# Row sums of attention weights by two adding transfers instead of matmuls with ones, and a new place for what uses them

## The chip, the cores and the metric

The kernel runs on one core of a Trainium2 chip. The time is that of the device, in microseconds, of one execution of the whole program; the median of three runs stands for a kernel. A core has TensorE (PE in the profile, with its weight loads as PEld), VectorE (DVE), ScalarE (ACT), GpSimd (POOL) and SyncE (SP), which here issues the transfers. Each engine works through its own list of instructions in order; they wait for each other through semaphores. Sixteen DMA engines move data between the on-chip memory and the device memory.

## The reference

Two layers over `x` of 16 batches, 1024 rows, 256 columns, all in float32. The first layer multiplies by a normalised adjacency matrix, then has two dense products with batch norms, a residual sum and a layer norm. The second, which the change is in, is attention:

```python
c_adj = jnp.mean(fea, axis=1)                     # of the rows, fea = x transposed
diff = c_adj[:, None, :] - c_adj[:, :, None]
A = jnp.abs(jnp.abs(jax.nn.sigmoid(diff) - 0.5) - 0.5) * 2.0
A_s = (A + jnp.transpose(A, (0, 2, 1))) * 0.5
g = jnp.einsum('bcn,bnm->bcm', fea, adj[None, :, :] * A_s)
q = relu(g * para)                                # in 4 heads of 64
k, v = x @ kv_w                                   # in 4 heads of 64
attn = jax.nn.softmax(jnp.einsum('bhnd,bhmd->bhnm', q, k) * scale, axis=-1)
out = jnp.einsum('bhnm,bhmd->bhnd', attn, v)
x = _layernorm(x + out, axis=-1)
```

The softmax needs, for each query and head, the sum of 1024 exponentials. That sum is what the change computes in another way.

## The kernel before: the parts concerned

The attention stage goes through 256 steps `g`, 16 a batch. Four steps make a turn; a turn is one half of the queries (`hf`, 512 of them) with one pair of heads, so a batch has four turns. A step makes scores for two blocks of 128 keys (`s`), takes their exponentials (`e`), adds these into `acc` and multiplies them by the values (`o`):

```python
def scores(g):
    ...
        t = ps_s.tile([P, 2, FB], F32, tag="s", name=f"s{g}_{a}")      # two buffers, a step fills both
        ... nc.tensor.matmul(t[...], kTs[...], qTs[...], start=True, stop=True)

def exps(g):
    for a in range(2):
        E[g, a] = ep.tile([P, 2, FB], F32, tag="e", name=f"e{g}_{a}")  # six buffers
        nc.scalar.activation(E[g, a], S.pop((g, a)), AF.Exp)

def sums(g):
    ...
    if cp == 0:
        ACC[b, hf, pair] = accp.tile([P, 2, FB], F32, tag="acc", name=f"acc{g}")
        nc.vector.tensor_add(ACC[b, hf, pair], E[g, 0], E[g, 1])
    else:
        for a in range(2):
            nc.vector.tensor_add(ACC[b, hf, pair], ACC[b, hf, pair], E[g, a])
```

`acc` then still has 128 partial sums, one a partition, for each query and head. `dens` adds them with matmuls by a block of ones, once per half, in the first matmuls of the next turn:

```python
def dens(b, hf):
    p = ps_t.tile([P, FB], F32, tag="t", name="pd")
    for pair in range(NP):
        acc = ACC.pop((b, hf, pair))
        for h in range(2):
            k = 32 * (2 * pair + h)
            ... nc.tensor.matmul(p[k : k + 32, :], ones32, t[:, h, :], ...)
    DT[b, hf] = otp.tile([P, FB], F32, tag="dt", bufs=1, name=f"dt{b}_{hf}")
    nc.scalar.copy(DT[b, hf], p)
    if not by_pe(b, hf):
        for k in range(HEADS):
            put_o(b, hf, slice(C + k * DR, C + (k + 1) * DR), DT[b, hf][32 * k : 32 * k + DR, :])
```

The outputs and the sums (`DR = 8` equal rows a head) go to device memory and come back in blocks (`fetch_o`, tile `ob`), so that a transposition in 32x32 blocks brings them into rows. `finish_a` does that for 256 queries (in this text: a finished pair, of two row blocks), divides, adds the residual and takes the moments; `finish_b` normalises and stores:

```python
def finish_a(b, j):
    ...
        t = pool_r[0].tile([P, 2, CD], F32, tag=pool_r[1], name=f"r_{b}_{j}")       # CD = C + HEADS * DR
        nc.vector.transpose(
            t.rearrange("p a c -> p (a c)"), OB.pop((b, j)).rearrange("p a c -> p (a c)")
        )
        nc.vector.reciprocal(rd, t[:, :, C:].rearrange("p a (h r) -> p a h r", r=DR)[:, :, :, 0])
        p = r = t[:, :, :C]
    ...
        nc.vector.tensor_mul(r..., p..., rd...)
    nc.vector.tensor_add(r, r, x1s.pop((b, j)))
    mv, rs = ln_stats(sm, r, f"z{b}_{j}")
    ...
```

The first layer's result for later batches is prepared in the same turns: `bn2_q` (GpSimd, tile `yt`), `rows` and `ln1_a` (VectorE: `x`, `mv_a`; then GpSimd: `rs_a`, `nm_a`), `ln1_b` (ScalarE, `x`). Keys (`pk`), values (`pv`) and the graph product (`pg`, whose results become `qT`) of the next batch fill TensorE at the front of a turn.

A table says at which half turn each piece is put out: `put(b, t, f, ...)` at half turn `t` of batch `b` (eight a batch), `between[k]` after step `k`. The pieces of both half turns stand ahead of the turn's steps:

```python
for t in range(...):
    g = NK * t
    now = [p for s in (2 * t, 2 * t + 1) for p in [(opening, (s,))] + arrange(at.get(s, []))]
    behind = max((k + 1 for k, fa in enumerate(now) if is_short(fa)), default=0)
    for k in range(len(now) + 1):
        if k == behind and 0 <= g < nsteps:
            sums(g)
        if k < len(now):
            f, a = now[k]
            f(*a)
    for k in range(g, g + NK):
        if 0 <= k + 1 < nsteps:
            scores(k + 1)
            exps(k + 1)
        if 0 <= k < nsteps:
            if k > g:
                sums(k)
            attend(k)
        for f, a in between.pop(k, ()):
            f(*a)
```

`dens` is one of the short pieces, so in a turn with `dens` the first addition `sums(g)` stands behind it.

Of the kernel before, what the change touches and what calls it, by code (L numbers as in the profile page):

```python
# [9 lines left out]
F32 = mybir.dt.float32  # L10
AF = mybir.ActivationFunctionType
OP = mybir.AluOpType
AX = mybir.AxisListType
# [3 lines left out]
P = 128  # L17
# [5 lines left out]
def gnn_norm_attention_kernel(  # L23
# [16 lines left out]
    nc = tc.nc  # L40
    B, N, C = x.shape
# [5 lines left out]
    NH = N // FB  # L47
# [33 lines left out]
    Q = 32  # L81
# [1 line left out]
    y_blk = [yT_all[b].rearrange("i (d e) (q n) -> q e (i d) n", e=Q, q=NQ) for b in range(B)]  # L83


    DR = 8
    CD = C + HEADS * DR
    o_dram = {(b, h): dram.tile([NT // NH, CD, P], F32, name=f"o{b}_{h}") for b in range(B) for h in range(NH)}
    x1_dram = {
# [39 lines left out]
    with ExitStack() as l0:  # L129
# [33 lines left out]
        with ExitStack() as ph1:  # L163
# [9 lines left out]
            for i in range(0, NT, 2):  # L173
                t = hp.tile([P, 2, N], F32, tag="h", name=f"A{i}")
# [29 lines left out]
            for h in range(NH):  # L204
                rows = range(h * KB, (h + 1) * KB)
# [10 lines left out]
                for j in range(NT):  # L216
                    p = ps.tile([P, FB], F32, tag="ah"[j % 2], name="pat")
                    for k, i in enumerate(rows):
                        nc.tensor.transpose(p[:, ts(k, P)], A[i][:, ts(j, P)], ident)
                    dst, acc = AhT[:, j, ts(h, FB)], col[:, h, j : j + 1]  # L220
# [22 lines left out]
            for c in range(HT):  # L243
                p = ps.tile([P, FB], F32, tag="a", name="pw1")
# [3 lines left out]
            for c in range(CT):  # L248
                p = ps.tile([P, FB], F32, tag="a", name="pw2")
# [149 lines left out]
            for f in range(HT):  # L399
                for h in range(NH):  # L400
# [3 lines left out]
                    p = hidden(B - 1, h, f)  # L404
# [5 lines left out]
        right = lambda name, bufs: ctx.enter_context(tc.tile_pool(name=name, bufs=bufs, side="right"))  # L410
        keep = right("keep", 1)
        ldp = right("ldp", LDP)
        accp = right("accp", 2)
        RD = keep.tile([P, B * NT + 1, HEADS], F32, name="RD")
        ones32 = keep.tile([P, 32], F32, name="ones32")
        stq = keep.tile([P, 2, C // Q], F32, name="stq")
# [45 lines left out]
        with ExitStack() as ph2:  # L462
# [69 lines left out]
            for f in range(KF, HT):  # L532
                t = hT[u][:, f, :]
# [29 lines left out]
    NP = HEADS // 2  # L563
# [17 lines left out]
    def fast():  # L581
      with ExitStack() as fx:
# [9 lines left out]
        otp = pool("otp", 3)  # L592
# [235 lines left out]
        def by_pe(b, hf):  # L828
            return b == B - 1 and hf == NH - 1

        def attend(g):
            b, hf, pair, cp = step(g)
            if cp == 0:
                O[b, hf, pair] = [ps_t.tile([P, FB], F32, tag="t", name=f"o{g}_{r}") for r in range(2)]
            for a in range(2):
                cb = 2 * cp + a
                for r in range(2):
                    for h in range(2):
                        nc.tensor.matmul(  # L839
                            O[b, hf, pair][r][h * HD : (h + 1) * HD, :],  # L840
                            vs[b][r * HD : (r + 1) * HD, cb, pair * P + h * HD : pair * P + (h + 1) * HD],
                            E[g, a][r * HD : (r + 1) * HD, h, :],
                            start=(cb == 0),
                            stop=(cb == NT - 1),
                        )
                E.pop((g, a))
            if cp == NT // 2 - 1:
                t = otp.tile([P, FB], F32, tag=f"ot{pair}", bufs=1, name=f"ot{g}")
                o = O.pop((b, hf, pair))
                nc.scalar.copy(t, o[0])  # L850
                nc.vector.tensor_add(t, o[1], t)  # L851
                if by_pe(b, hf):
                    OT[b, hf, pair] = t
                else:
                    put_o(b, hf, slice(pair * P, (pair + 1) * P), t)

        def put_o(b, hf, rows_, t):
            nc.sync.dma_start(
                o_dram[b, hf][:, rows_, :].rearrange("i p n -> p i n"), t.rearrange("p (i n) -> p i n", n=P)
            )  # L860
# [50 lines left out]
        def finish_a(b, j):  # L911
            hf, k = divmod(2 * j, KB)
            pool_r = (rp, "r") if b < B - 1 or not by_pe(b, hf) else (x1p, "x1")
            rd = RD[:, b * NT + 2 * j : b * NT + 2 * j + 2, :]
            if by_pe(b, hf):
                r = pool_r[0].tile([P, 2, C], F32, tag=pool_r[1], name=f"r_{b}_{j}")
                p = OB.pop((b, j))
            else:
                t = pool_r[0].tile([P, 2, CD], F32, tag=pool_r[1], name=f"r_{b}_{j}")
                nc.vector.transpose(  # L920
                    t.rearrange("p a c -> p (a c)"), OB.pop((b, j)).rearrange("p a c -> p (a c)")
                )
                nc.vector.reciprocal(rd, t[:, :, C:].rearrange("p a (h r) -> p a h r", r=DR)[:, :, :, 0])
                p = r = t[:, :, :C]
            if j == NT // 2 - 1 and by_pe(b, hf):

                for a in range(2):
                    for h in range(HEADS):
                        nc.scalar.mul(r[:, a, ts(h, HD)], p[:, a, ts(h, HD)], rd[:, a, h : h + 1])
            else:  # L930
                nc.vector.tensor_mul(
                    r.rearrange("p a (h d) -> p a h d", h=HEADS),
                    p.rearrange("p a (h d) -> p a h d", h=HEADS),
                    rd.unsqueeze(3).to_broadcast([P, 2, HEADS, HD]),
                )
            nc.vector.tensor_add(r, r, x1s.pop((b, j)))
            mv, rs = ln_stats(sm, r, f"z{b}_{j}")
            nm = sm.tile([P, 2], F32, tag="nm", name=f"nm_{b}_{j}")
            for a in range(2):
                nc.gpsimd.tensor_scalar(  # L940
                    nm[:, a : a + 1], mv[:, a, 0:1], rs[:, a : a + 1], -1.0, op0=OP.mult, op1=OP.mult
                )
            R[b, j] = (r, rs, nm)
# [43 lines left out]
        def put(w, t, f, *a):  # L987
            at.setdefault(w * NC + t, []).append((f, a))
# [4 lines left out]
        for b in range(B):  # L993

            for hf in range(NH):
                t = (hf + 1) * (NC // NH)
                put(b, t, dens, b, hf)
                if by_pe(b, hf):
                    put(b, t, recips, b, hf)
                for k in range(KB // 2):  # L1000
                    j = hf * (KB // 2) + k

                    if b * NH + hf < B * NH - 3:
                        t_f, t_a, t_b = (t + 1, t + 2 + k, t + 6 + k) if hf == 0 else (t + 1, t + 4 + k, t + 6 + k)
                    elif not by_pe(b, hf):

                        t_f, t_a, t_b = t, t + 2 * k, t + 2 + 2 * k if b < B - 1 else (t + 2, NC + 1)[k]
                        if b == B - 1 and k == 0:
                            between[(b * NC + t_b) * 2 + NK // 2] = [(finish_b, (b, j))]
                            t_b = None  # L1010
                    else:
                        t_f, t_a, t_b = t, t + 1 + k, t + 2 + k
                    put(b, t_f, back if by_pe(b, hf) else fetch_o, b, j)
                    if t_a == t:
                        between[(b * NC + t) * 2 + NK // 2] = [(finish_a, (b, j))]
                    else:
                        put(b, t_a, finish_a, b, j)
                    if t_b is not None:
                        put(b, t_b, finish_b, b, j)
            if b == 0:  # L1020
                continue

            if b > 1:
                put(b - 2, 2, begin, b)
                for j in range(NT // 2):
                    put(b - 2, j, load, b, j)
                    put(b - 2, j + 1, bn2_q, b, j)
                    put(b - 2, j + 2, rows, b, j)
                    put(b - 2, j + 2, ln1_a, b, j)
                    put(b - 2, j + 3, ln1_b, b, j)  # L1030
                    put(b - 2, j + 3, put_x1, b, j)
                    put(b - 2, 5 + j // 2 * 2, get_x1, b, j)
                    put(b - 2, min(6 + j, NC), x1_v, b, j)
                put(b - 2, NC - 2, means, b)
                put(b - 2, NC - 1, crow, b)

            i = 0
            for t, n in enumerate(WG):
                for i in range(i, i + n):
                    put(b - 1, t, gate, b, i)  # L1040
                i += 1
            kv = [(keys, (b, c, h)) for h in range(NH) for c in range(CT)]
            kv += [(values, (b, j)) for j in range(0, NT, 2)]
            for t, n in enumerate(KV):
                for _ in range(n):
                    f, a = kv.pop(0)
                    put(b - 1, t, f, *a)
            m = 0
            for t, n in enumerate(QG):
                for m in range(m, m + n):  # L1050
                    put(b - 1, NC - len(QG) + t, graph, b, m)
                m += 1
# [3 lines left out]
        nsteps = B * NS  # L1056


        order = (dens, recips, x1_t, finish_a, fetch_o, finish_b, x1_v, rows, ln1_a, ln1_b, put_x1, get_x1, means, load, crow)
        rank = {f: k for k, f in enumerate(order)}  # L1060
        short = (dens, recips, x1_t, back)

# [15 lines left out]
        def arrange(pieces):  # L1078
            first = []
            gates = [fa for fa in pieces if fa[0] is gate]  # L1080
            many = [fa for fa in pieces if fa[0] in long]
            first += [fa for fa in pieces if fa[0] is bn2_q]
            alone = [fa for fa in pieces if fa[0] in (dens, back, recips, crow)]
            few = [fa for fa in pieces if fa not in first + gates + many + alone]
# [305 lines left out]
```

## Time and profile before

| | |
|---|---|
| time, median of 3 | 2456.35 us (2456.02 to 2457.38) |
| span of the profiled execution | 2454.0 us, 33894 instructions |
| TensorE busy | 2411.8 us, 98% |
| VectorE busy | 1811.3 us, 74% |
| ScalarE, GpSimd busy | 1094.8 us (45%), 776.9 us (32%) |
| DMA | 292.73 MB, 119 GB/s on average |
| attention stage, per batch | 100.5 us (1172.40 to 1272.92, and the like) |

How to read it: busy time is an average over stages that differ. What one piece of work is worth is read from the stretch it stands in: whether TensorE has gaps there, and which instruction released it. A group's line gives the program's line, engine, operation, the tile written and the tiles read, shapes and count, then the busy time, the mean of one, and the idle time of the engine just before with what ended it. Two or more matmuls on different parts of the array overlap, so their mean durations do not add up to the busy time. Each float32 matmul stands in the records as two passes.

### The profile page before, as it was taken

The numbers are of one execution on the slowest core, as the hardware profiler recorded it, in microseconds if no ns is written. First come the engines' busy times: TensorE is split into PE (matmuls) and PEld (weight loads), VectorE is DVE, ScalarE is ACT, GpSimd is POOL, SyncE is SP. The second block draws the span as 40 slices with busy tenths as digits, with TensorE's granted clock in tenths as the row PEclk, the third lists the DMA queues.
The fourth block names the chain that finished last, engine by engine and source line by source line (L and its number), as shares of the span: only waits on it lengthen the run. The fifth ranks groups of instructions, "written<-read, shape, count | busy, mean of one in ns | idle before, by whom it ended". The sixth has DMA issues, their size and how long they took to land. (4 is left out here: it accounts for less than half of the span.)

```text
span 2454.0 us, 33894 instructions
## 1 busy us (share of the span) xinstructions
PE 2411.8 (98%) x12225; PEld 1008.5 (41%) x12225; DVE 1811.3 (74%) x2584; ACT 1094.8 (45%) x1555; POOL 776.9 (32%) x826
## 2 busy tenths in 40 slices
PE   8999999999999899999999999999999999999997
PEld 4444444444344443443434434344343443443432
DVE  5555545556776777888788888888888888888677
ACT  2000000001554455564655646656566565564645
POOL 2222222231556521414224133232332323414013
PEclk9999999999999899999999999999999999999999
DMA  3122122222578543544545545545354453544222
GB/s 137 69 86 103 69 86 103 85 87 86 199 272 278 133 121 83 143 119 112 143 106 129 143 95 146 122 120 144 81 150 114 123 149 89 145 112 118 72 44 56
DMA packets 583951, 292.73 MB, mean 119 GB/s; under 512 B 407528, under 2 KB 556512, under 8 KB 576608
## 3 DMA queue, kind: packets, MB, share of 16 engines
q1 hardware_dynamic: 583776, 290.49, 43.0%
q8 instruction: 98, 1.61, 0.3%
q14 instruction: 77, 0.63, 0.1%
HBM read 194.46 MB, written 95.94 MB: 118 GB/s over the span
## 5 line engine op out<-in xcount | busy, mean ns | idle before, releaser
L809 ACT ACTIVATE e<-s 128x1024 f32<-128x1024 f32 x512 | 496.0, 1020 | 327.5 <-PE s L797 265.4
L824 DVE TENSOR_TENSOR acc<-acc,e 128x1024 f32<-128x1024 f32 x382 | 509.3, 1333 | 112.1 <-ACT e L809 85.4
L797 PE MATMUL s<-qT,kT 64*64 64x512 f32 x4096 | 490.7, 594 | 4.4 <-ACT e L809 1.7
L839 PE MATMUL o<-e,v 64*64 64x512 f32 x4096 | 485.3, 589 | 0.0
L771 PE MATMUL pg<-wg,x 128*128 128x512 f32 x960 | 426.5, 597 | 0.0
L624 POOL TENSOR_TENSOR yt<-yt,stq 128x512 f32<-128x512 f32 x120 | 185.2, 1544 | 406.4 <-DMA yt<-yT 239.8
L771 PEld LDWEIGHTS pg<-wg,x 128*128 128x128 f32 x960 | 178.7, 190 | 238.6 <-issue 237.4
L839 PEld LDWEIGHTS o<-e,v 64*64 64x64 f32 x4096 | 156.6, 133 | 282.9 <-issue 275.2
L797 PEld LDWEIGHTS s<-qT,kT 64*64 64x64 f32 x4096 | 147.1, 133 | 298.5 <-issue 254.2
L107 ACT COPY u<-pa 128x512 f32<-128x512 f32 x15 | 8.8, 586 | 475.3 <-PE pa L313 475.3
L66 POOL TENSOR_SCALAR rs_z<-mv_z 128x2 f32<-128x2 f32 x64 | 18.5, 290 | 470.5 <-DVE mv_z L573 470.4
L730 DVE SCALAR_TENSOR_TENSOR wg<-wg,adj 128x1024 f32<-128x1024 f32 x128 | 163.4, 1308 | 2.8
L313 PE MATMUL pa<-AhT,x 128*128 128x512 f32 x360 | 161.8, 592 | 0.0
L656 ACT ACTIVATE x<-x,nm_a,rs_a 128x256 f32<-128x256 f32 x128 | 75.8, 594 | 171.9 <-POOL nm_a L646 171.4
L851 DVE TENSOR_TENSOR ot<-o,ot 128x512 f32<-128x512 f32 x64 | 44.2, 691 | 127.5 <-ACT ot L850 127.5
L757 PE MATMUL pv<-kvw,x1T 128*128 128x256 f32 x512 | 118.7, 385 | 0.0
L746 PE MATMUL pk<-x1T,kvw 128*128 128x512 f32 x256 | 117.9, 604 | 0.0
L66 POOL TENSOR_SCALAR rs_a<-mv_a 128x2 f32<-128x2 f32 x64 | 38.0, 594 | 236.5 <-DVE mv_a L573 235.2
L344 PE MATMUL ph<-agg,SW 128*128 128x512 f32 x240 | 112.8, 592 | 0.0
L757 PEld LDWEIGHTS pv<-kvw,x1T 128*128 128x128 f32 x512 | 97.1, 192 | 31.8 <-issue 16.2
L313 PE MATMUL pa<-T,sx 128*128 128x512 f32 x240 | 107.9, 592 | 0.0
L313 PEld LDWEIGHTS pa<-AhT,x 128*128 128x128 f32 x360 | 68.4, 190 | 86.1 <-issue 86.1
(198 smaller groups left out, 3147.1 us busy)
## 6 DMA issues: line engine op xcount, KB each, us to landing
adj<-in_adj_dram SPq DMA_DIRECT2D x128, 512.0 KB
h<-hT SPq DMA_DIRECT2D x28, 1024.0 KB
hL<-h SPq DMA_DIRECT2D x28, 1024.0 KB
ob<-o SPq DMA_DIRECT2D x248, 72.0 KB
x<-in_x_dram SPq DMA_DIRECT2D x16, 1024.0 KB
yT<-y SPq DMA_DIRECT2D x64, 256.0 KB
out_dram<-r SPq DMA_DIRECT2D x64, 256.0 KB
xr<-in_x_dram SPq DMA_DIRECT2D x62, 256.0 KB
```

Of the source, the lines that this page charges most:

```text
L313: nc.tensor.matmul(p, xs[n][:, k, :], bs[n][:, k, :], start=(k == 0), stop=(k == KN - 1))
L344: nc.tensor.matmul(p, ws[n][:, ts(f, P)], bs[n], start=True, stop=True)
L624: nc.gpsimd.tensor_tensor(y, y, sc, op)
L656: nc.scalar.activation(r, r, AF.Identity, bias=nm[:, a : a + 1], scale=rs[:, a : a + 1], accum_out=css[b][:, i : i + 1])
L730: nc.vector.scalar_tensor_tensor(t, t, 1.0, adjs[b * NT + i], op0=OP.add, op1=OP.mult)
L746: nc.tensor.matmul(p, kvw[:, k, ts(c, P)], x1Ts[b][:, k, ts(h, FB)], start=(k == 0), stop=(k == CT - 1))
L757: nc.tensor.matmul(p[:, ts(a, C)], x1Ts[b][:, k, ts(j + a, P)], kvw[:, k, C:], start=(k == 0), stop=(k == CT - 1),)
L771: nc.tensor.matmul(pg[b], x1s[b, k // 2][:, k % 2, ts(c, P)], wgs[b, k][:, ts(h, FB)], start=(k == 0), stop=(k == NT - 1))
L797: nc.tensor.matmul(t[r * HD : (r + 1) * HD, h, :], kTs[b, pair][h * HD : (h + 1) * HD, ts(2 * cb + r, HD)], qTs[b, pair, hf][h * HD : (h + ...
L809: nc.scalar.activation(E[g, a], S.pop((g, a)), AF.Exp)
L824: nc.vector.tensor_add(ACC[b, hf, pair], ACC[b, hf, pair], E[g, a])
L839: nc.tensor.matmul(O[b, hf, pair][r][h * HD : (h + 1) * HD, :], vs[b][r * HD : (r + 1) * HD, cb, pair * P + h * HD : pair * P + (h + 1) * HD],
```

## The change

For 29 of the 32 halves (all but the last three; `by_dma`) the matmuls with ones go away. In their place each `acc` is folded by two adding transfers issued from GpSimd: partitions 64 to 127 are added onto 0 to 63, then 32 to 63 onto 0 to 31. The 32 rows left go to device memory (`put_den`, after the third step of the turn), so that the block transposition puts the 32 partial sums of a query side by side, and VectorE adds them. The aim is to take work off TensorE. `accp` has a third buffer, since an `acc` now lives a turn longer; `DR` is 32 instead of 8. The two folds are put out one in each half turn, first of all its pieces. The finished pairs of the first half go to the last turn of their batch, one within the pieces and one after the first step; those of the second half to the next batch's second turn (after its second step) and third turn (in the pieces). The sums are fetched at three places: the front of the last turn, the end of the next batch's first turn, the middle of the pieces of its second.

```diff
-    DR = 8
+    DR = Q                                   # Q = 32
...
-        accp = right("accp", 2)
+        accp = right("accp", 3)
...
+        def by_dma(b, hf):
+            return b * NH + hf < B * NH - 3
+
+        def fold(b, hf, pair, n):
+            acc = ACC[b, hf, pair]
+            nc.gpsimd.dma_start(acc[:n], acc[n : 2 * n], accum_op=OP.add)
+
+        def put_den(b, hf, pair):
+            acc = ACC.pop((b, hf, pair))
+            for h in range(2):
+                r = C + (2 * pair + h) * DR
+                put_o(b, hf, slice(r, r + DR), acc[:DR, h, :])
...
-                t = pool_r[0].tile([P, 2, CD], F32, tag=pool_r[1], name=f"r_{b}_{j}")
-                nc.vector.transpose(
-                    t.rearrange("p a c -> p (a c)"), OB.pop((b, j)).rearrange("p a c -> p (a c)")
-                )
-                nc.vector.reciprocal(rd, t[:, :, C:].rearrange("p a (h r) -> p a h r", r=DR)[:, :, :, 0])
-                p = r = t[:, :, :C]
+                p = r = pool_r[0].tile([P, 2, C], F32, tag=pool_r[1], name=f"r_{b}_{j}")
+                den = otp.tile([P, 2, CD - C], F32, tag="den", bufs=1, name=f"den_{b}_{j}")
+                ob = OB.pop((b, j))
+                nc.vector.transpose(den, ob[:, :, C:])
+                nc.vector.transpose(r, ob[:, :, :C])
+                den = den.rearrange("p a (h r) -> p a h r", r=DR)
+                if by_dma(b, hf):
+                    nc.vector.tensor_reduce(rd, den, AX.X, OP.add)
+                    nc.vector.reciprocal(rd, rd)
+                else:
+                    nc.vector.reciprocal(rd, den[:, :, :, 0])
...
-                put(b, t, dens, b, hf)
+                if by_dma(b, hf):
+                    for pair in range(NP):
+
+                        s = b * NC + t + 2 * (pair - NP + 1)
+                        for k in range(2):
+                            put(0, s + k, fold, b, hf, pair, P // 2 >> k)
+                        between.setdefault(2 * s + 2, []).append((put_den, (b, hf, pair)))
+                else:
+                    put(b, t, dens, b, hf)
...
                     if b * NH + hf < B * NH - 3:
-                        t_f, t_a, t_b = (t + 1, t + 2 + k, t + 6 + k) if hf == 0 else (t + 1, t + 4 + k, t + 6 + k)
+                        t_f, t_a, t_b = t + 2 + k * hf, t + 3 + hf, t + 6 + k
+
+                        if k != hf:
+                            t_a = None
+                            between.setdefault((b * NC + t + 2) * 2 + hf, []).append((finish_a, (b, j)))
+                        if hf == 1 and k == 0:
+                            t_f = None
+                            between.setdefault((b * NC + t) * 2 + NK - 1, []).append((fetch_o, (b, j)))
...
+            first += [fa for fa in pieces if fa[0] is fold]
             first += [fa for fa in pieces if fa[0] is bn2_q]
```

More of the change, by code (lines that the diff above doesn't have):

```diff
@@ L1008, in fast @@
                         if b == B - 1 and k == 0:
-                            between[(b * NC + t_b) * 2 + NK // 2] = [(finish_b, (b, j))]
+                            between.setdefault((b * NC + t_b) * 2 + NK // 2, []).append((finish_b, (b, j)))
                             t_b = None
@@ L1012, in fast @@
                         t_f, t_a, t_b = t, t + 1 + k, t + 2 + k
-                    put(b, t_f, back if by_pe(b, hf) else fetch_o, b, j)
+                    if t_f is not None:
+                        put(b, t_f, back if by_pe(b, hf) else fetch_o, b, j)
                     if t_a == t:
-                        between[(b * NC + t) * 2 + NK // 2] = [(finish_a, (b, j))]
-                    else:
+                        between.setdefault((b * NC + t) * 2 + NK // 2, []).append((finish_a, (b, j)))
+                    elif t_a is not None:
                         put(b, t_a, finish_a, b, j)
@@ L1056, in fast @@
         nsteps = B * NS
-        order = (dens, recips, x1_t, finish_a, fetch_o, finish_b, x1_v, rows, ln1_a, ln1_b, put_x1, get_x1, means, load, crow)
+        order = (dens, recips, x1_t, put_den, finish_a, fetch_o, finish_b, x1_v, rows, ln1_a, ln1_b, put_x1, get_x1, means, load, crow)
         rank = {f: k for k, f in enumerate(order)}
```

## The prediction

> **What bounds the kernel now.** I read the busy times first, then busy times by stretch, then single groups, then one turn in order of time. The page's first part:
>
> ```profile
> PE 2411.8 (98%) x12225; PEld 1008.5 (41%) x12225; DVE 1811.3 (74%) x2584; ACT 1094.8 (45%) x1555; POOL 776.9 (32%) x826
> ```
>
> TensorE is busy 98% of the span. A batch in the attention stage is four turns; I call them A, B, C, D. Their edges are where a matmul that is neither a score nor an output follows an output (o) matmul. The stretches of one batch (columns: busy time of PE, PEld, DVE, ACT, POOL, clock, DMA share, GB/s):
>
> ```profile
> core 0: us, PE busy (x) PEld busy (x) DVE busy (x) ACT busy (x) POOL busy (x), PEclk, DMA share, GB/s
> 1172.40:1196.70 24.30, 24.17 (x164) 9.15 (x161) 20.28 (x18) 18.65 (x22) 5.56 (x4) 1.00 0.70 168
> 1196.70:1224.56 27.86, 27.86 (x177) 13.05 (x173) 23.05 (x27) 17.23 (x24) 11.25 (x12) 1.00 0.56 151
> 1224.56:1248.42 23.86, 23.86 (x160) 8.58 (x156) 21.85 (x38) 11.49 (x18) 9.48 (x16) 1.00 0.44 84
> 1248.42:1272.92 24.50, 24.50 (x157) 9.36 (x153) 19.53 (x33) 11.74 (x18) 4.11 (x8) 1.00 0.33 86
> ```
>
> PE has no gap in B, C and D and 0.13 us in A, so a matmul taken away shortens the kernel by its whole length unless another engine then comes late. VectorE is next: 84.7 of 100.5 us over the batch, and 21.85 of 23.86 us in C. Groups the change touches (busy, mean ns of one, idle before):
>
> ```profile
> L870 PE MATMUL pd<-acc,ones 128*32 128x512 f32 x256 | 36.1, 604 | 0.0
> ...
> L824 DVE TENSOR_TENSOR acc<-acc,e 128x1024 f32<-128x1024 f32 x382 | 509.3, 1333 | 112.1 <-ACT e L809 85.4 <-DVE acc L824 0.9
> ...
> L920 DVE STREAM_TRANSPOSE r<-ob 128x576 f32<-128x576 f32 x62 | 47.6, 768 | 2.0 <-DMA ob<-o 2.0
> ```
>
> The timeline of turn C (start, length, engine, what, idle before):
>
> ```profile
> 1224.56 1.12 PE L771 MATMUL pg<-wg,x 128*128 128x512 f32 x2
> ...
> 1225.61 1.07 PE L870 MATMUL pd<-acc,ones 128*32 128x512 f32 x8
> ...
> 1232.04 0.18 DVE L573 BATCH_NORM_AGGREGATE mv_a<-st_a 128x2 f32<-128x6 f32 x1
> ...
> 1232.38 1.03 POOL L66 TENSOR_SCALAR rs_a<-mv_a 128x2 f32<-128x2 f32 x1 [1.00 <-DVE mv_a L573]
> ...
> 1234.53 1.95 PE L797 MATMUL s<-qT,kT 64*64 64x512 f32 x16
> ...
> 1235.15 0.60 ACT L656 ACTIVATE x<-x,nm_a,rs_a 128x256 f32<-128x256 f32 x1 [7.80 <-POOL nm_a L646]
> 1236.48 1.92 ACT L809 ACTIVATE e<-s 128x1024 f32<-128x1024 f32 x2
> 1238.01 1.47 PE L797 MATMUL s<-qT,kT 64*64 64x512 f32 x12
> ```
>
> The reader should see a chain that is nearly tight. VectorE's moments of the rows two batches ahead (mv_a) go through GpSimd (rs_a, nm_a) to ScalarE (x), which is in front of the exponentials e in ScalarE's order. The score tiles have two buffers and a step fills both, so the next scores, at 1238.01, need the first exponential read. It ends near 1236.48 + 0.97 = 1237.45 (half of a 1.94 us pair elsewhere): 0.55 us to spare.
>
> [...] two acc additions beside GpSimd's yt at 1212.54 took 3.78 us (VectorE timeline at 1212.88), two without it 2.55 us (at 1264.68).
>
> **The change, part by part.** *Removed:* 29 of the 32 dens (all but the last three halves): 8 passes of pd, one ScalarE copy (0.59 us) and four 16 KB stores each. In C, pg, pd and pg together fill 1224.56 to 1234.53, 9.97 us, with 20 passes of pg. The 24 passes of turn D run from 1248.42 to 1258.83, 0.434 us each, so 20 take 8.68, and some 0.09 for the turn to the scores (0.52 us between the last pg and the first s instead of 0.43). pd[...] costs 9.97 - 8.77 = 1.2 us, twice a batch. 29 x 1.2 = 35 us, all on PE's path: 2456 - 35 = 2421 us is the floor.
>
> *Added on GpSimd and DMA:* 58 pairs x 2 folds. A fold waits for the last addition (at the front of the next turn), the second for the landing of the first[...]. The sums are put out after the third step of that turn, some 17 us after its start, so SyncE should not be held. Stores of the sums grow from 64 to 256 KB a half, fetches (ob) from 288 to 384 KB a pair. DMA is busy 33% to 70% by turn, and ob was fetched a turn ahead: no cost expected.
>
> *Added on VectorE:* per pair one transposition of 576 columns (0.768) and a reciprocal (0.204) become transpositions of 512 (0.709, as x<-yt) and 256, a reduction and the reciprocal. From 576 and 512 columns a transposition grows 0.92 ns a column: 0.47 us for 256. Reductions took 1.214 us for 1024 columns and 0.642 for 480, 1.05 ns a column: 0.41 for 256. 0.71 + 0.47 + 0.41 + 0.20 - 0.97 = 0.82 us more, so a finished pair takes 3.66 (1225.89 to 1229.55) + 0.82 = 4.5 us. 58 x 0.82 = 48 us on an engine with 16 us to spare a batch: hidden on average, but not where it falls.
>
> *Moved:* the pairs of the first half go to turn D of their batch, those of the second to B (after the second step) and C of the next. And because nothing short stands at the front of a turn any more, the first addition of a turn (acc<-e,e, 1.19 us) now precedes a finished pair and the new rows; before, it followed both in C. The order of instructions of the changed kernel shows both.
>
> Turn B: the second step's additions end at 1216.66, B + 20.0. Then the pair, 4.5, to 24.5; four more additions at 1.33 to 29.8. B is 27.86 long, so VectorE enters C 1.9 us late, where before it started the ot addition at C + 0.72. Turn C: ot 0.6, acc 1.2, pair 4.5, new rows 2.64 (1229.58 to 1232.22): mv_a is ready at C + 10.8, before at C + 7.7. The rest of the chain is unchanged: mv_a to the end of the first exponential took 1237.45 - 1232.22 = 5.2 us, so that end moves to C + 16.0. PE, without pd, wants it at 13.45 - 1.2 = C + 12.25. It waits 3.8 us. This needs a pair of the batch before and rows two ahead, so it comes in 13 batches: 13 x 3.8 = 49 us.
>
> In D and A I find little: pairs in D leave VectorE level at the turn's end (4.5 x 2 replace 3.66 x 2, of 19.5 in 24.5), in A the two x1T transpositions come 1.2 us later behind acc, costing PE about 0.3 us, and the 0.3 us that PE waits for ScalarE in A now (scores at 1186.18, 2.03 after the outputs instead of 1.72) goes away with the dt copy.
>
> Sum: 2456 - 35 + 49 = 2470 us.
>
> **Rivals.** *No new wait.* VectorE catches up in B, or the GpSimd steps after mv_a shrink: rs_a took 1.03 us at 1232.38 but 0.22 at 1207.23[...]. Then PE stays the bound and the time is 2421 to 2430. For it: VectorE's average leaves room, and placing one pair in C instead of two looks made for that. Against it: the second pair of C never stood ahead of mv_a. *GpSimd is held.* The yt of the fourth rows (3 us) moves from 1219.70 in B to behind the fold in C[...]. One microsecond more in C makes 2483, two 2496. *DMA or SyncE becomes late* through the longer fetches in D just before their use: 1 us a batch would add 14; the distance of several us speaks against it.
>
> **Range and chances.** The wait in C at two thirds, no wait at a quarter, something worse for the rest. The middle of that is somewhat below the sum: 2466 us, range 2424 to 2492. A gain over 2% needs less than 2407, below the floor of 2421: 0.02. A loss over 2% needs more than 2505, 2.7 us a batch beyond my sum: 0.05. Within 2%: 0.93.
>
> **What would show it.** Right: pd shrinks from 256 records to 24 on acc (its 8 on e stay); C is about 26.4 us long (23.86 - 1.2 + 3.8), its second scores start about 7 us after the first instead of 3.48, waiting for ScalarE's e, which waits for nm_a; B keeps 27.86, A is near 23.1, D 24.5. Wrong: C of 22.7 us and a batch of 98.1 (no wait); SyncE or the additions waiting for folds; PE gaps in A (x1T late) or D (ob late).

## The result and the profile after

The changed kernel takes 2491.31 us (2488.51 to 2496.12), the kernel before 2456.18 us (2455.00 to 2457.38), medians of four runs each. The ratio is 1.0145, with a 95% interval of 1.0127 to 1.0163: slower by about 35 us. The first part of the page shows what the change took from TensorE and that this did not shorten the span:

```profile
PE 2397.4 (96%) x11993; PEld 1005.7 (40%) x11993; DVE 1832.7 (74%) x2704; ACT 1079.7 (43%) x1526; POOL 883.5 (35%) x942
```

TensorE is busy 96% of the span now; it waits. The same four turns A, B, C, D of a batch in the changed kernel (busy time of PE, PEld, DVE, ACT, POOL, then granted clock, DMA share, GB/s):

```profile
1178.09:1201.78 23.69, 23.21 (x157) 9.00 (x153) 20.12 (x19) 18.26 (x21) 6.08 (x6) 1.00 0.70 172
1201.78:1229.63 27.85, 27.85 (x176) 13.07 (x173) 24.15 (x36) 17.22 (x24) 11.90 (x15) 1.00 0.83 195
1229.63:1257.24 27.61, 24.60 (x152) 8.83 (x149) 22.03 (x34) 10.78 (x17) 13.42 (x19) 0.94 0.38 70
1257.24:1281.74 24.50, 24.50 (x157) 9.36 (x153) 19.40 (x36) 11.73 (x18) 7.24 (x9) 1.00 0.72 138
```

B and D are what they were. In C TensorE is busy 24.60 of 27.61 us, and the clock's mean over the turn is 0.94. The groups of the changed work (busy, mean ns, idle before):

```profile
L839 POOL DMA_DIRECT2D acc<-acc x116 | 99.1, 854 | 413.9 <-DVE acc L824 312.8 <-DMA acc<-acc 101.1
...
L821 DVE TENSOR_TENSOR acc<-e,e 128x1024 f32<-128x1024 f32 x64 | 99.2, 1550 | 1.2 <-ACT e L809 1.2
...
L886 PE MATMUL pd<-acc,ones 128*32 128x512 f32 x24 | 5.2, 604 | 0.2 <-DVE acc L824 0.2
```

The records of matmuls with ones on `acc` fell from 256 to 24 (8 a half, two a matmul; side by side, with 604 ns each in the mean and 5.2 us busy in all). A fold holds GpSimd for 0.85 us. Counted from its issue it landed after 4.1 us (256 KB) and 3.6 us (128 KB) in the median. The first addition of a turn takes 1.22 us in most turns, much as before, but 2.85 to 2.87 us in 13 of the 15 turns C, where it took 1.19 us before; this makes the mean of 1.55.

The whole difference can be laid out by turns. The table gives sums over the batches of the attention stage from its first B on (14 A, 15 C; B and D, 417.8 and 367.4 us, did not change in any run), the first turn after them (the last batch's, "last turn"), and the time from the last edge between turns to the end of the span ("end"). The turns are cut at the edges that the prediction defines. The one turn between the last turn and the last edge takes 26.9 us in both kernels.

| kernel | A | C | last turn | end | time |
|---|---|---|---|---|---|
| before | 340.2 | 358.0 | 30.6 | 18.0 | 2456.2 |
| after | 335.4 | 388.7 | 33.7 | 23.9 | 2491.3 |
| difference | -4.8 | +30.7 | +3.1 | +5.9 | +35.1 |

The timeline of C in the changed kernel, with C's start at 1229.63 (start, length, engine, what, idle before):

```profile
1230.97 0.68 DVE L867 TENSOR_TENSOR ot<-o,ot 128x512 f32<-128x512 f32 x1
1231.35 0.91 POOL L839 DMA_DIRECT2D acc<-acc  x1 [0.25 <-DVE acc L824]
1231.57 2.87 DVE L821 TENSOR_TENSOR acc<-e,e 128x1024 f32<-128x1024 f32 x1
1232.02 3.32 POOL L624 TENSOR_TENSOR yt<-yt,stq 128x512 f32<-128x512 f32 x2
1234.36 0.43 DVE L938 STREAM_TRANSPOSE den<-ob 128x256 f32<-128x256 f32 x1
...
1241.04 0.18 DVE L573 BATCH_NORM_AGGREGATE mv_a<-st_a 128x2 f32<-128x6 f32 x1
...
1241.38 0.22 POOL L66 TENSOR_SCALAR rs_a<-mv_a 128x2 f32<-128x2 f32 x1 [1.00 <-DVE mv_a L573]
...
1242.85 0.60 ACT L656 ACTIVATE x<-x,nm_a,rs_a 128x256 f32<-128x256 f32 x1 [11.35 <-POOL nm_a L646]
...
1244.03 1.91 ACT L809 ACTIVATE e<-s 128x1024 f32<-128x1024 f32 x2
...
1245.08 1.96 PE L797 MATMUL s<-qT,kT 64*64 64x512 f32 x8 [3.01 <-ACT e L809]
```

Read it from the end: the scores of the next step waited 3.01 us for the exponential e, which stood in ScalarE's list behind x, which waited for GpSimd's nm_a, which needs mv_a from VectorE. mv_a is ready at C + 11.6 us, before at C + 7.7. Ahead of it on VectorE now stand the addition (2.87 us) and the finished pair (from den to the last moments, 4.21 us). Thirteen turns C have such a wait. In seven of them the turn takes 25.3 to 26.0 us; in six, this one among them, TensorE also runs at a slower clock after the wait (0.50 granted, for 3.41 us, in one of them 6.83 us), and the turn takes 27.0 to 29.1 us.

### The profile page after: what moved, and what is told of

Same layout as the page of the kernel before. It is cut to its first block, busy times and chain, and to the rows that moved or that the text cites. A ratio compares the mean times of both kernels' runs of the same rounds, so it can differ in the third digit from the quotient of the medians.

```text
span 2489.1 us, 33793 instructions
## 1 busy us (share of the span) xinstructions
PE 2397.4 (96%) x11993; PEld 1005.7 (40%) x11993; DVE 1832.7 (74%) x2704; ACT 1079.7 (43%) x1526; POOL 883.5 (35%) x942
## 5 line engine op out<-in xcount | busy, mean ns | idle before, releaser
L824 DVE TENSOR_TENSOR acc<-acc,e 128x1024 f32<-128x1024 f32 x382 | 479.9, 1256 | 106.7 <-ACT e L809 78.3
L797 PE MATMUL s<-qT,kT 64*64 64x512 f32 x4096 | 503.3, 607 | 39.9 <-ACT e L809 37.1
L839 POOL DMA_DIRECT2D acc<-acc x116 | 99.1, 854 | 413.9 <-DVE acc L824 312.8
L624 POOL TENSOR_TENSOR yt<-yt,stq 128x512 f32<-128x512 f32 x120 | 175.4, 1462 | 89.9 <-DMA yt<-yT 74.4
L66 POOL TENSOR_SCALAR rs_z<-mv_z 128x2 f32<-128x2 f32 x64 | 41.1, 642 | 364.1 <-DVE mv_z L573 333.3
```

Of the source, the lines that this page charges most:

```text
L624: nc.gpsimd.tensor_tensor(y, y, sc, op)
L797: nc.tensor.matmul(t[r * HD : (r + 1) * HD, h, :], kTs[b, pair][h * HD : (h + 1) * HD, ts(2 * cb + r, HD)], qTs[b, pair, hf][h * HD : (h + ...
L839: nc.gpsimd.dma_start(acc[:n], acc[n : 2 * n], accum_op=OP.add)
```

## Experiments

The theory: two orders on VectorE cost the time, the first addition ahead of the short work in A and C, and the finished pair ahead of the rows in C. The rivals: the folds hold GpSimd (or what else needs it); or the new places and wider transfers are the loss whatever their order. Each run is compared with runs of the kernel before on its own chip (2455.3 to 2455.5 us). All changes are against the changed kernel unless said otherwise.

**The first addition put back (x1_late_add).**

```diff
             behind = max((k + 1 for k, fa in enumerate(now) if is_short(fa)), default=0)
+            if t > 0 and t % 2 == 0:
+                behind = max(behind, 1 + len(arrange(at.get(2 * t, []))))
```

> The changed kernel with one thing undone: in turns A and C the first addition of a turn (acc<-e,e) is put back behind the first half turn's pieces, as it stood before. Theory 1, the loss is a chain on VectorE in turn C (and x1T in turn A): the addition, 2.87 us in C, leaves the way of mv_a, so TensorE's wait of 3 us for the first exponential shrinks to under 1 us, the slow clock after it goes, and A goes from 24.0 to about 23.1; 15 x (1.2 to 3.5) in C and 14 x 0.75 in A less: 2445 to 2460 us. Rival 1, the folds hold GpSimd or its engines' data: the folds stay, so 2485 to 2491. Rival 2, the new places of the finished pairs are the whole cost: the pair stays ahead of the rows, so also 2485 or more.

2453.94 us, ratio to before 0.9994 (0.9985 to 1.0003): 37 us less than the changed kernel. A is 323.9 in sum, 23.1 a turn but for two turns up to 0.3 longer: the loss in A is gone whole. C is 362.7, and the slow clock is gone from it (mean granted clock of the profiled execution 0.992, in the changed kernel 0.988). What is left in C, a wait of about 1.4 us in most batches, must come from the pair, since it still stands ahead of the rows.

**GpSimd's yt ahead of the fold (x2_yt_first).**

```diff
-            first += [fa for fa in pieces if fa[0] is fold]
             first += [fa for fa in pieces if fa[0] is bn2_q]
+            first += [fa for fa in pieces if fa[0] is fold]
```

> The changed kernel with GpSimd's yt put out ahead of the fold in each turn instead of behind it. Theory 1 with contention as a part of it: the addition in C took 2.87 us beside yt and takes 1.2 to 1.3 when yt has ended or starts earlier; TensorE's wait in C shrinks by 1.6 us and the slow clock[...] goes too: C near 24 us, 2450 to 2468 in all.[...] Rival 1 (the fold itself is late): the fold lands 3 us later, so slower, 2495 to 2510.

2466.28 us, ratio 1.0045 (1.0030 to 1.0061). C falls from 388.7 to 366.7 in sum, A stays (334.8). In C the same two instructions now lie like this:

```profile
1224.68 3.03 POOL L624 TENSOR_TENSOR yt<-yt,stq 128x512 f32<-128x512 f32 x2
...
1225.20 1.61 DVE L821 TENSOR_TENSOR acc<-e,e 128x1024 f32<-128x1024 f32 x1
```

The addition takes 1.61 us instead of 2.87. It lies beside yt in both kernels; what differs is which of the two starts first. In the changed kernel the issue of the fold (0.91 us) puts the start of yt 0.44 us behind that of the addition, here yt starts 0.52 us ahead of it. Why this order makes so much difference is not shown. In C the fold thus costs TensorE time by moving another GpSimd instruction against VectorE's critical one.

**The pair behind the rows (x3_pair_late).**

```diff
-                        t_f, t_a, t_b = t + 2 + k * hf, t + 3 + hf, t + 6 + k
+                        t_f, t_a, t_b = t + 2 + k * hf, t + 3 + 2 * hf, t + 6 + k
```

> The changed kernel with the one finished pair that stands in turn C moved from ahead of the rows to behind them (the first addition stays at the front). Theory 1: mv_a comes over 4 us earlier, TensorE does not wait in C and keeps its clock: C 22.7 us each, 340 in sum instead of 389; A, the end and the drain keep their costs: 2440 to 2448 us. Rival 1 (folds hold GpSimd): GpSimd's list is the same, 2480 or more. Rival 2 (the pair only moves its load elsewhere in C): VectorE enters D late and D grows by what C loses, 2475 or more.

2452.76 us, ratio 0.9989 (0.9980 to 0.9997). C is 22.68 in all 15 batches, without a wait, though the addition ahead of the rows still takes 2.57 to 2.87 us. But A grew from 335.4 to 347.9: the expectation took A as unchanged, and it was not. VectorE now enters A later (ot starts at A + 1.73 instead of A + 0.87 in the third batch of the stage), and TensorE waits for the transposed x1T. The waits of TensorE for x1T and of VectorE for ob over the whole program (us in total, times, longest), first in the changed kernel:

```profile
PE pk L746 <- DVE x1T L679: 7.5, 12, 1.5
DVE den L938 <- DMA ob<-o: 48.6, 17, 3.9
```

then with the pair behind the rows:

```profile
PE pk L746 <- DVE x1T L679: 17.7, 13, 2.6
DVE den L938 <- DMA ob<-o: 59.4, 17, 5.0
```

So 12 of the 49 us come back in another turn, but not as the rival put it, by a load that only moves: VectorE stands idle in D, for the blocks ob that the first finished pair of D reads. Behind that wait its list in D runs on without a gap into the next turn. The end of the wait and the entry into the next A, in the changed kernel (D starts at 1257.24, A at 1281.74):

```profile
1265.16 0.45 DVE L938 STREAM_TRANSPOSE den<-ob 128x256 f32<-128x256 f32 x1 [3.03 <-DMA ob<-o]
...
1282.88 0.68 DVE L867 TENSOR_TENSOR ot<-o,ot 128x512 f32<-128x512 f32 x1
```

In all 14 pairs of D and A of the changed kernel, ot starts in A at the length of this wait less 1.90 us (here 3.03 and 1.14). With the pair behind the rows the wait in D is 3.7 us in the median instead of 2.95, and ot comes that much later.

**No folds (x5_no_fold).** It leaves out the addition of 96 of the 128 partial sums of each query and head; stores, fetches and all else stay.

```diff
-            nc.gpsimd.dma_start(acc[:n], acc[n : 2 * n], accum_op=OP.add)
+            return
```

> The changed kernel without its adding transfers; everything else, the stores and fetches of 32 rows a head too, stays. It leaves out the addition of 96 of the 128 partial sums. Theory 1: the pair and the addition still stand ahead of the rows, only the addition is less in contention, since yt starts 1 us earlier: 1 to 2 us less of wait in C, and the 9.5 us of GpSimd's last drain go, worth about 6 us: 2450 to 2475. Rival 1 (folds and GpSimd are the cost): all goes, 2421 to 2430. Rival 2 (placement alone): 2480 to 2491.

2454.54 us, ratio 1.0001 (0.9990 to 1.0012). The folds therefore cost 37 us of the changed kernel, but not all 70 us between it and the floor of 2421. In the profiled executions, 33.2 us apart, C gives back 22.4, A 5.6 and the end 5.0. In C this is the same as with yt ahead of the fold (366.3 and 366.7): the folds' part there is the place of yt beside the addition. In A it is ob: VectorE's wait for it is shorter without folds,

```profile
DVE den L938 <- DMA ob<-o: 35.6, 17, 2.8
```

and ot starts at A + 0.72 in 13 of the 14 turns, against 0.87 to 2.04 with folds. What stays without folds is the part of the two orders: C is 26 us above 15 turns of 22.68, and A 6 us above 14 turns of 23.1.

**Both orders (x4_late_add_pair_late).** The edits of the first and third runs together.

> The changed kernel with both moves of the first set at once: the first addition of turns A and C behind the first half turn's pieces, and the finished pair of C behind the rows. Theory 1 (two orders on VectorE cost the time; each move alone gave about 37 us): C 22.68 us as with the pair late, A 23.1 to 23.4 as with the addition late, last turns and the 9.5 us of GpSimd's drain as they are: 2489 - 49 - 11 = 2426 to 2434 us. Rival (the work only moves: with both behind, VectorE's list is full and A grows to 24.5 or more, as it did with the pair alone): 2444 to 2455.

2430.88 us, ratio 0.9899 (0.9884 to 0.9914). C is 22.68 in all batches, A 324.6 in sum. The rival that A would stay long falls: with the addition behind, x1T comes in time in all but two turns, although VectorE still waits for ob in D. Placing both pieces right turns a loss of 1.5% into a gain of 1.0%, with every fold still there.

**One transfer in the kernel before (x6_before_one_fold).** Against the kernel before:

```diff
+        probe = keep.tile([P, 32], F32, name="probe")
+        nc.vector.memset(probe, 0.0)
+        nc.gpsimd.dma_start(probe[:64], probe[64:], accum_op=OP.add)
```

> The kernel before with a single adding transfer of 8 KB on a scratch tile at the start of the program. If GpSimd's last drain has a fixed price once the program has such a transfer: a drain of about 9.5 us at the end and a time 5 to 6 us above before (2460 to 2462). If the drain grows with the number of the transfers (116 in the changed kernel) or is the last one's own completion: a drain of under 0.2 us, and no difference.

2455.84 us, ratio 1.0001 (0.9993 to 1.0009). The end of the program holds three instructions DRAIN of GpSimd. Their durations (ns, shortest/median/longest of three), in the kernel before, in this one, and in the changed kernel:

```profile
L1385 POOLq DRAIN  x3: 34/50/82, 2449.0 to 2453.7; - x3
```

```profile
L1388 POOLq DRAIN  x3: 34/93/139, 2449.9 to 2455.0; - x3
```

```profile
L1423 POOLq DRAIN  x3: 34/98/9538, 2478.7 to 2488.8; - x3
```

The longest is the first of the three in the last two kernels (in the kernel before the first took 50 ns). One transfer adds 89 ns, 116 add 9488 ns, 82 ns each: not a fixed price.

**Matmuls with ones kept (x9_dens_kept).**

```diff
-            return b * NH + hf < B * NH - 3
+            return False
```

> The changed kernel with the sums made by the matmuls with ones as before; the new places of the finished pairs and the fetches, 32 rows a head and the two transpositions stay, no adding transfer. With pd among the pieces the first addition falls behind it again. Theory 1: no drain (-6), A near 24.3, and in C the pair alone is ahead of the rows, mv_a at about C + 9 and the first exponential at C + 14.2, wanted at 13.45, a wait of up to 1 us in 13 batches: 2456 to 2470. Rival 2 (the new places and the wider transfers are the loss by themselves): 2480 or more. If C shows no wait, 2454 to 2458.

2457.65 us, ratio 1.0010 (1.0003 to 1.0016). With `pd` in the turn the first addition falls behind it, and C is 358.6, only 0.5 us more than before in 15 batches. New places, 32 rows a head, two transpositions and a longer fetch together cost 2 us. The rival that places and transfers are the loss by themselves falls. This run has no folds either. So what costs is what happens when `pd` goes: TensorE comes 1.2 us earlier and the addition comes to the front, which is the loss of the run without folds (C at 366.3, A at 329.8), and the folds add theirs.

**A late normalisation at the end (x7_late_end).** Both orders, and:

```diff
-                        if b == B - 1 and k == 0:
+                        if k == 0:
                             between.setdefault((b * NC + t_b) * 2 + NK // 2, []).append((finish_b, (b, j)))
```

> The fourth run's kernel (both moves) with one more: at the last batch, the normalisation of the last finished pair but one of the batch before (two ScalarE activations, r<-r,nm,rs_z) goes from ahead of the second turn's exponentials to behind its second step. Theory: it takes the place of the wait of 3.2 to 3.4 us before the scores and the slow clock after it, seen in every variant at that turn (33.7 to 35 us against 30.6): 29 to 30.6 us there, 4 us less than without it. If those two wait for the same four others of ScalarE anyway, 1 us or less.

2426.85 us, ratio 0.9883 (0.9868 to 0.9898). The last turn takes 29.0 instead of 33.7 us. In the changed kernel ScalarE had four normalisations in one row ahead of the exponentials there (2.08 us, after a wait of 1.98 us for nm), and TensorE waited 3.18 us. A batch of this kernel, turns A to D:

```profile
1167.03:1190.14 23.11, 22.98 (x157) 9.08 (x153) 19.25 (x19) 18.27 (x21) 7.15 (x6) 1.00 0.74 177
1190.14:1217.99 27.85, 27.85 (x176) 13.07 (x172) 24.04 (x37) 17.23 (x24) 12.55 (x16) 1.00 0.90 195
1217.99:1240.67 22.68, 22.68 (x153) 8.52 (x149) 20.61 (x33) 10.80 (x17) 13.24 (x18) 1.00 0.44 82
1240.67:1265.17 24.50, 24.50 (x158) 9.36 (x154) 19.53 (x36) 11.73 (x18) 7.46 (x10) 1.00 0.68 140
```

The sum is 98.14 us, of which TensorE is busy 98.01: this is the batch that the prediction gave for "no wait". VectorE does the same work as in the changed kernel, in another order.

**Folds in half of the batches (x8_half_folds).** The last kernel without the folds of batches 8 to 15; it leaves out the same additions there.

```diff
             acc = ACC[b, hf, pair]
+            if b >= B // 2:
+                return
```

> The last kernel (both moves and the late end) without the adding transfers of batches 8 to 15, 64 of 116 are left; it leaves out the addition of 96 of 128 partial sums in those batches. The last transfer is then some 700 us before the end. If GpSimd's drain grows with their number (9.49 us more for 116, 0.09 more for 1): 5.2 to 5.3 us, and the end 2 to 4 us shorter than 22.67. If it waits for the last ones: under 0.2 us. If it has a fixed price above a few: about 9.5 us. The turns should stay 22.67, 24.50, 23.11 and 27.86 with and without transfers, since TensorE has no wait there to lose: 2422 to 2425 us.

2422.35 us, ratio 0.9867 (0.9851 to 0.9884). The drain:

```profile
L1427 POOLq DRAIN  x3: 34/98/5292, 2413.7 to 2419.5; - x3
```

That is 5242 ns above the 50 of the kernel before, for 64 transfers: 82 ns each again, although the last one is far back (in the changed kernel the 64th is issued 782 us ahead of the drain). A is 324.1 and C 340.1, as with all folds: in these orders a fold costs TensorE nothing in a turn, and the only price seen is at the end, which is 18.7 us long instead of 22.7 with all folds.

## Why the prediction was right and where it was wrong

**The time.** 2491.31 us lies inside the range of 2424 to 2492, but at its very edge, by less than the runs differ among themselves (2488.51 to 2496.12); that it lies inside is luck. 2466 was 25 us low. The sum of 2470 lacked three terms: 12 us in A, 6 at the end, 3 in the last turn.

**The floor: right.** The 1.2 us that the prediction gives for `pd` is measured twice: C without waits is 22.68 instead of 23.87, A without waits 23.10 instead of 24.30. The best kernel with all sums in place takes 2427 us, 6 us above the floor of 2421; its end is 4.7 us longer than before.

**The wait in C: the chain right, the size by luck.** The chain came as predicted, from the pair and the addition over mv_a, nm_a and x to e and the scores. "13 x 3.8 = 49 us": against 15 turns of 22.68 the changed kernel has 48.5 us more. But TensorE's waits are 2.4 to 3.3 us, 33.9 in 13 turns. The rest is a slower clock in six turns, 9.7 us, of which the prediction says nothing (last section), and 4.9 us that are not split further. The terms of the 3.8 us also differ from the step as put:

- "VectorE enters C 1.9 us late": ot starts at C + 0.72 in 8 of the 13 turns, as before, and at C + 0.80 to 1.61 in the others (1.34 in the turn shown). In the turn shown the pair took 4.22 us in B instead of 4.5, and the four additions after it 1.30 each instead of 1.33.
- "acc 1.2": it took 2.87 beside yt. The prediction has both parts of this, two additions beside yt at 3.78 instead of 2.55 us and yt moved into C in the rival "GpSimd is held", which it took as an alternative; it is a part of the outcome, and the runs x2_yt_first and x5_no_fold show it.
- "mv_a to the end of the first exponential 5.2 us": 3.8 (1241.22 to about 1245.0 in the turn shown), mostly as rs_a took 0.22 instead of 1.03 us.
- The pair took 4.21 instead of 4.5 us, and TensorE wanted the exponential at C + 12.44 instead of 12.25. For a turn that VectorE enters on time the sum is then 3.8 - 1.2 + 1.7 - 0.3 - 1.4 - 0.2 = 2.4 us, the shortest wait that is measured.

**A: wrong.** The step that failed: x1T "1.2 us later behind acc, costing PE about 0.3 us", cancelled by "the 0.3 us that PE waits for ScalarE". The gain did not come: the second scores start 2.03 us after the first outputs in every A, before and after. The cost was larger: A without a wait is 23.1, without folds it is 23.54, and measured is 24.0 on average, 12 us in 14 turns. Before, `pd` (1.07 us) stood between the first pk matmuls and the next and covered the time in which x1T was made. Without it the next pk came forward, while the addition sent x1T back: this is 0.4 us a turn, 6 of the 12 us, and with the addition behind, as in x1_late_add, the wait is gone. The other 5.6 us need the folds. By the traces they come from D, where ob lands later and VectorE then enters A later (x3_pair_late and x5_no_fold above). Whether the folds' own transfers hold up the fetch there is not shown: they run at the same time, and no run moves them apart.

**The end: missed.** The first DRAIN of 9.54 us begins after GpSimd's last instruction, while stores and the other engines' ends run beside it. So the end grew by 5.9 us and not by 9.5; 5.0 of it goes with the folds (23.9 and, without them, 19.0). That 82 ns a transfer add up there was not foreseen. The last turn's 3.1 us were also missed, since those halves keep their matmuls and were taken as unchanged. There TensorE waits 3.18 us instead of 1.68, and the 16 score passes after it take 3.64 us instead of 2.00. The run x7_late_end shows that two normalisations less ahead of the exponentials remove this. But they stood there before too; in the traces the moments that they need are ready only 0.6 us ahead of the scores of the step before, instead of 1.9, and that this makes the difference was not tested.

**The rivals.** "No new wait" was wrong for this kernel, but describes the best one. "DMA or SyncE becomes late": it came true in part, in a place where it was not looked for. VectorE waits 48.6 us for ob in all, before 2.0; D stays at 24.50, but by A it has reached TensorE, as said. The prediction's "no cost expected" for the transfers holds without folds: with the matmuls kept VectorE waits 36.7 us for ob, and A stays at 24.30. VectorE's extra work per pair, put at 0.82 us, was smaller (a pair took 4.21 us in C, 4.22 in B, before 3.66): the 256-column transposition took 0.44 and the reduction 0.37, near the estimates of 0.47 and 0.41.

## What to carry to other kernels

A matmul that is taken off a full TensorE is only worth its length if what TensorE does next is ready that much earlier: look for what it had been covering (here x1T and the moments of the next rows), and put that work first on its engine. A rule of order that hangs on the removed piece (here "the addition behind the short pieces") must be set anew. An issue on an engine off the path is not free if it shifts a neighbour against an instruction on the path (here a fold of 0.91 us shifted yt, and the addition beside it took 2.87 instead of 1.19 us). With new transfers, look again at the fetches whose readers feed TensorE a turn later (VectorE waited 48.6 us for ob with folds, 35.6 without), and at the end of the program, where a cost per transfer may fall due (here a drain of 9.54 us for 116).

## What the hardware showed that was not expected

**The clock after a short wait.** In the changed kernel two waits of 2.39 us in C, one followed by a slow clock and one not: the stretch of 3.41 us with the wait, and the one after it (columns as for the turns; the clock is the third number from the right):

```profile
2265.75:2269.16 3.41, 1.02 (x16) 0.14 (x11) 3.10 (x9) 2.31 (x6) 2.94 (x6) 1.00 0.36 34
2269.16:2272.57 3.41, 3.41 (x20) 1.02 (x24) 2.73 (x3) 1.80 (x2) 2.48 (x2) 0.50 0.70 140
1651.35:1654.76 3.41, 1.62 (x16) 0.31 (x8) 3.22 (x8) 1.65 (x5) 2.61 (x7) 1.00 0.11 11
1654.76:1658.17 3.41, 2.82 (x28) 1.01 (x32) 3.06 (x4) 3.04 (x4) 3.10 (x3) 1.00 0.81 140
```

After the first wait the 16 score passes took 3.64 us, after the second 1.99. Of the 13 waits in C, of 2.39 to 3.27 us, six were followed by a clock of 0.50; the longest that was not took 3.04 us, so the length alone did not tell. In the traces of the two kernels, before and changed, from 100 us on, the slow stretches begin whole multiples of 3.413 us from one another and, but for the one at the end of the program, last 3.413, 6.827 or 13.653 us. In steps of 3.413 us counted from them, each of the 13 at full clock in which TensorE was busy for at most 0.300 of the time was followed by a clock of 0.50, and none of the other 1351, all with 0.44 or more. This is worked out from the recorded clock and from matmul records whose ends are modelled. What sets the clock is not shown. It was slow where the waits were: in the run with both orders (x4_late_add_pair_late), where C has no wait, the mean granted clock of the profiled execution is 0.993, in the changed kernel 0.988, in the kernel before 0.995. No run made or stopped it by itself.

**The closing DRAIN of GpSimd** took 0.05 us without adding transfers and 0.139, 5.292 and 9.538 us with 1, 64 and 116 of them: 82 to 89 ns each. What GpSimd does in that time the profile does not show.
